# A factorization-machine kernel on one core: the bias addition moves from VectorE to ScalarE and GpSimd, and one transfer of squares is asked for four slots later

## The chip, the cores and the metric

The kernel runs on one core of one Trainium2 chip. The metric is the device time of one execution in microseconds; the time before is the median of 3 runs. A profile is one further execution, taken by the hardware profiler. The engines are named as in the profile: PE is TensorE (PEld its weight loads), DVE is VectorE, ACT is ScalarE, POOL is GpSimd, SP is SyncE. GpSimd and SyncE also ask for DMA transfers; a transfer asked for by GpSimd stands in GpSimd's own order of instructions.

## What is computed

A batch of 1024 vectors of 512 features goes through a linear layer and through 64 embedding matrices of 512 x 512; the squares of the products are summed over the 64 matrices, and a second term with squared inputs and weights is taken off:

```python
out_lin = x @ lin_w.T + lin_b
xv = jnp.einsum('bf,efm->bem', x, weight)
zp = jnp.einsum('bf,efm->bem', jnp.square(x), jnp.square(weight))
interaction = 0.5 * jnp.sum(jnp.square(xv) - zp, axis=1)
return out_lin + interaction
```

All of it is float32. The kernel keeps twice the result, `2 * (x @ lin_w.T + lin_b) + sum of squares`, in two accumulators and takes the half at the end, which is why the bias enters doubled.

## The kernel before

**Tiling.** The 64 matrices are worked through in 16 blocks of four (q = 0 to 15). Products are formed by a two-level fast scheme with seven products instead of eight. The outer level has seven operand matrices "1", "2", "6", "7", "5", "3", "4" for each block, in this order (`UNITS`). Each of them has two column halves j = 0, 1, and each such unit (line 413) makes seven inner products on TensorE, "1", "5", "6", "2", "7", "3", "4", into three PSUM banks x, v and y. A block has thus 7 x 2 x 7 = 98 products, each of them two profiled matmul pieces of 128x512.

**Slots and order.** Everything is put into one list with a due time in slots (`st.at(t, fn)`), sorted by it and then issued in that order, by hand. One slot is one inner product, a block takes 98 slots, and block q starts at slot 98q. Each engine runs its own instructions in that order; a fraction of a slot only sets the order. So an instruction that waits holds back all later ones of its engine, and for GpSimd that includes the transfers it asks for.

**What GpSimd does.** It forms the differences of weights for the scheme: outer ones on line 380 (`outer_t`), inner ones on lines 391, 393 and 395 (`inner_t`, called tp, t6 and t4 in this order for each operand matrix). TensorE reads these. On line 472 (`rest`) it does additions of 128x1024 for operand "5", at slots 67 and 69.8 of a block for j = 0, and 74 and 76.8 for j = 1; these wait for VectorE's last `join` (line 467) into tile s. On line 506 (`gather`) it asks for the transfers that add squares from z tiles into an accumulator, and on line 522 for those that sum squared weights.

**What VectorE does.** It takes the products out of PSUM: lines 446, 457, 458 and 467 each add a bank and an SBUF tile. TensorE writes the banks again, so it waits for these reads: product "4" goes into bank y after `join("y", 3)` on line 467 has read it.

**Accumulators and squares.** The result has four blocks of quarters, named by z tiles: place "a", "b" and "c" (`place`, line 407). ScalarE squares them in place (line 497). The accumulators `acc0` and `acc1` are 128 x 2 x 2 x 512 each, indexed by j, then by column half s. In each block these transfers go into them (slot in the block, j, half u of the tile):

- c into acc0: 38.8 (u 0) and 52.9 (u 1), both j together, 1024 KB each
- c into acc1: 73 and 84 (j 0), 80 and 91.5 (j 1), 512 KB each
- a into acc0, called C12 in the change: 88 (j 0, u 0), 96.5 (j 1, u 0), 99.5 (j 0, u 1), 110.3 (j 1, u 1), 512 KB each
- b into acc1: 111.3 and 124.2, both j together, 1024 KB each

A number above 98 falls into the next block. Each transfer reads and writes the accumulator, so one into a part waits until the earlier one into the same part has landed: 99.5 waits for 88. The last block has its own ending for a and b (lines 741 to 751). Places a and c change their tiles with each block, so a tile that holds a in one block is written as c by VectorE in the next.

**The bias.** A row of 512 numbers is loaded to all partitions (line 350, 256 KB). The addition on VectorE, line 348, is one operation for each accumulator, j and s: eight in all, two in each of blocks 1 to 4, at slots 27.6 (acc0) and 41.6 (acc1):

```python
for n in range(4):
    for r, t in enumerate((27.6, 41.6)):
        st.at(98 * (n + 1) + t, lambda r=r, n=n: add_bias(r, n // 2, n % 2))
```

Of the kernel before, what the change touches and what calls it, by code (L numbers as in the profile page):

```python
# [9 lines left out]
AF = mybir.ActivationFunctionType  # L10
ALU = mybir.AluOpType
# [17 lines left out]
def kernel(  # L29
# [31 lines left out]
    nc = tc.nc  # L61
    _, _, _, Q = x.shape
    E, F, M = weight.shape
    P = 128
# [16 lines left out]
    acc = [  # L81
        const.tile([P, 2, 2, M], F32, tag=f"acc{r}", name=f"acc{r}") for r in range(2)
    ]
# [26 lines left out]
    st = Stream()  # L110
# [232 lines left out]

    bias = const.tile([P, M], F32, tag="bias", name="bias")

    def add_bias(r, j, s):
        o = acc[r][:, j, s]
        nc.vector.scalar_tensor_tensor(o, bias, 2.0, o, ALU.mult, ALU.add)  # L348

    st.at(-1, lambda: nc.sync.dma_start(bias, lin_b.partition_broadcast(P)))  # L350

    for n in range(4):
        for r, t in enumerate((27.6, 41.6)):
            st.at(98 * (n + 1) + t, lambda r=r, n=n: add_bias(r, n // 2, n % 2))

    def load_w(q, kk, v):
        src = weight[4 * q + 2 * v : 4 * q + 2 * v + 2]
        nc.sync.dma_start(
            WB[kk][v], src.rearrange("u (p k) m -> p u k m", k=NK)[:, :, ts(kk, 2)]
        )  # L360
# [12 lines left out]
    def outer_t(i, u):  # L373
        a, b = {
            "5": (WB[0][1], WB[0][0]),
            "6": (WB[1][1], T5),
            "7": (WB[1][1], WB[0][1]),
            "4": (WB[1][0], T6),
        }[i]
        nc.gpsimd.tensor_sub(OUTER[i][:, u], a[:, u], b[:, u])  # L380
# [3 lines left out]
    def inner_t(q, i, n):  # L384

        b = OUTER[i]
        k = 2 if n == "tp" else 1
        t = tpool.tile([P, k, M], F32, tag=n, name=f"{n}_{q}_{i}")
        TI[q, i, n] = t
        if n == "tp":  # L390
            nc.gpsimd.tensor_sub(t, b[:, 1], b[:, :, 0])  # L391
        elif n == "t6":
            nc.gpsimd.tensor_sub(t[:, 0], b[:, 1, 1], TI[q, i, "tp"][:, 0])
        else:
            nc.gpsimd.tensor_sub(t[:, 0], b[:, 0, 1], TI[q, i, "t6"][:, 0])  # L395
# [96 lines left out]
    def squares(t, q, n, j, wait):  # L492
        z = place(q, n)
        for u in range(2):
            st.at(
                t + max(wait, 0.1) * u,
                lambda u=u: nc.scalar.activation(z[:, u, j], z[:, u, j], AF.Square),  # L497
            )
# [3 lines left out]
    def gather(t, q, n, r, j, u):  # L502
        def fn():
            z = place(q, n)[:, u]
            o, z = (acc[r], z) if j is None else (acc[r][:, j], z[:, j])
            nc.gpsimd.dma_start(o, z, accum_op=ALU.add)  # L506

        st.at(t, fn)

    def w_squares(t, q, v, u):  # L510
        first = q == v == u == 0

        def sq(kk):
            o = (w2_sum if first else w2_sb)[:, ts(kk, 2)]
            nc.scalar.activation(o, WB[kk][v][:, u], AF.Square)

        for kk in range(2):
            st.at(t + 0.1 * kk, lambda kk=kk: sq(kk))
        if not first:
            st.at(  # L520
                t + (3.2 if t < 0 else 5),
                lambda: nc.gpsimd.dma_start(w2_sum, w2_sb, accum_op=ALU.add),
            )
# [11 lines left out]
    for q in range(NQ):  # L535
        g0 = 98 * q
        last = q == NQ - 1
        for kk, v, t in ((1, 0, -41), (0, 0, -37.5), (0, 1, -37), (1, 1, -3)):
            if q:
                st.at(g0 + t, lambda q=q, kk=kk, v=v: load_w(q, kk, v))  # L540

        for i, t0, t1 in (
            ("5", -9.9, 2) if q else ("5", -11, -10.9),
            ("6", 14.2, 14.3) if q else ("6", 0.5, 0.6),
            ("7", 28.7, 28.8),
            ("4", 50, 53),
        ):
            for u, t in enumerate((t0, t1)):
                st.at(g0 + t, lambda i=i, u=u: outer_t(i, u))
        for i, *times in (  # L550
            ("1", -6.4, -1.4, 2.1) if q else ("1", -11.5, -11.4, -11.3),
            ("2", 6.4, 6.5, 10.2) if q else ("2", -5, -4.9, -4.8),
            ("6", 20.7, 20.8, 27),
            ("7", 34.4, 34.5, 39.7),
            ("5", 43.1, 43.2, 43.3),
            ("3", 57.9, 58, 61.7),
            ("4", 81, 82.1, 84.1),
        ):
            for n, t in zip(("tp", "t6", "t4"), times):
                st.at(g0 + t, lambda q=q, i=i, n=n: inner_t(q, i, n))  # L560
        for n, (i, (addend, dst)) in enumerate(UNITS.items()):
            for j in range(2):
                unit(g0 + 14 * n + 7 * j, q, i, j, addend, dst)

        for k, n, r, times in (
            (1, "c", 0, ((None, 38.8), (None, 52.9))),
            (4, "c", 1, ((0, 73), (0, 84), (1, 80), (1, 91.5))),
            (5, "a", 0, ((0, 88), (0, 99.5), (1, 96.5), (1, 110.3))),
            (6, "b", 1, ((None, 111.3), (None, 124.2))),
        ):  # L570
            for j in range(2):
                t = g0 + 14 * k + 7 * j + 14.6
                squares(t - (0.95 if last and n == "b" else 0), q, n, j, 4 * (k == 4))
            for m, (j, t) in enumerate(times):
                if not last or n == "c":
                    gather(g0 + t, q, n, r, j, m % 2)
        if q == 0:
            w_times = (-6, 14.8, 37, 56.6)
        else:
            w_times = (-19.2, 14.8, 37, 56.6)  # L580
        for n, t in enumerate(w_times):
            w_squares(g0 + t, q, n // 2, n % 2)
# [249 lines left out]
```

## Time and profile before

| | |
|---|---|
| median of 3 runs | 1425.74 us (1425.23 to 1425.85) |
| profiled execution, its own time | 1423.9 us |
| span of the profile | 1422.1 us |
| granted TensorE clock, mean | 0.996 |
| VectorE busy, share of the span | 893.6 us, 63% |
| ScalarE busy, share of the span | 620.8 us, 44% |
| HBM read, written | 72.61 MB, 2.10 MB |
| line 348, eight operations | 1.37 to 5.67 us each, from 138.3 to 414.0 us |
| line 472, 64 operations | 2.36 us mean |
| line 506, waits for an earlier transfer | 62.7 us in 15 waits, the longest 4.8 |

The span is the time from the first to the last instruction of the profile; the execution's own time has a little more around it. "Busy" counts the time in instructions, so an instruction that is held up while it runs counts as busy too. A name such as `y L421 <- z L467` in a list of waits says: the instruction on line 421 that writes y waited for the one on line 467 that writes z. In a timeline each line has the start and the duration in us, the engine, the line of the kernel, the operation, output `<-` inputs, the shape, the count, and in brackets the idle time before it with what ended it.

### The profile page before, as it was taken

How to read it: one execution, taken by the hardware profiler on the slowest of the kernel's cores; microseconds unless marked ns; L12 is line 12 of the kernel's file. 1: busy time of each engine (PE TensorE's matmuls, PEld its weight loads, DVE VectorE, ACT ScalarE, POOL GpSimd, SP SyncE). 2: the span in 40 equal slices, each digit the busy share in tenths (PEclk: the TensorE clock that was granted, in tenths of full speed). 3: DMA queues.
4: the chain of work that ended last, by engine and by line, in shares of the span. 5: the costliest groups of instructions: out<-in, count | busy, mean ns of one | idle time of the engine just before them, and what ended most of it. 6: DMA issues, size and time to landing. Idle time of an engine off the chain costs nothing.

```text
span 1422.1 us, 11166 instructions
## 1 busy us (share of the span) xinstructions
PE 1407.7 (99%) x3340; PEld 636.5 (45%) x3340; DVE 893.6 (63%) x1271; ACT 620.8 (44%) x824; POOL 1248.8 (88%) x812
## 2 busy tenths in 40 slices
PE   9999999999999999999999999999999999999999
PEld 5444444444444444444444444444444444444446
DVE  6665667657576565665656566565666656566665
ACT  2444353443534435344443534534353443534443
POOL 7988789888898888979989898988989988898984
PEclk9999999999999999999999999999999999999999
DMA  5299898898888998997998899898998998899885
GB/s 214 59 222 191 200 197 160 200 195 195 197 163 206 196 206 193 182 238 156 230 195 197 204 181 234 166 232 178 191 233 160 225 195 211 186 184 237 163 189 133
DMA packets 58108, 273.63 MB, mean 192 GB/s; under 512 B 5440, under 2 KB 8000, under 8 KB 41792
## 3 DMA queue, kind: packets, MB, share of 16 engines
q0 software_dynamic: 36432, 198.20, 71.1%
q1 hardware_dynamic: 21328, 74.19, 15.3%
q10 hardware_dynamic: 288, 0.52, 0.1%
q8 instruction: 27, 0.44, 0.1%
q14 instruction: 33, 0.27, 0.1%
HBM read 72.61 MB, written 2.10 MB: 53 GB/s over the span
## 4 chain that ended last, share of the span: by engine, by line
PE 94%; DMA 2%; issue 1%; POOL 1%; DVE 1%; ACT 0%; POOLq 0%
PE y L421 39%; PE x L421 26%; PE v L421 25%; DMA acc<-z 2%; PE lin L216 1%; PE y_last L659 1%; DVE acc L348 1%; PE v_last L659 0%; PE x_last L659 0%; POOL t L380 0%; PE y_lin L271 0%; DMA t<-lin_wT 0%; POOL t L395 0%; PE v_lin L271 0%; PE x_lin L271 0%
## 5 line engine op out<-in xcount | busy, mean ns | idle before, releaser
L421 PE MATMUL y<-t,xs 128*128 128x512 f32 x896 | 424.0, 594 | 10.3 <-DVE z L467 9.6
L475 ACT COPY y<-x 128x512 f32<-128x512 f32 x224 | 127.7, 570 | 623.1 <-PE x L421 623.0
L467 DVE TENSOR_TENSOR z<-y,s 128x512 f32<-128x512 f32 x192 | 132.7, 691 | 238.0 <-PE y L421 238.0
L421 PEld LDWEIGHTS y<-t,xs 128*128 128x128 f32 x896 | 169.7, 190 | 226.7 <-issue 202.8
L506 POOL DMA_DIRECT2D acc<-z x190 | 213.2, 1153 | 64.3 <-DMA acc<-z 62.7
L497 ACT ACTIVATE z<-z 128x1024 f32<-128x1024 f32 x256 | 260.1, 1054 | 11.8 <-POOL z L472 9.3
L421 PE MATMUL x<-w,xs 128*128 128x512 f32 x512 | 252.0, 600 | 0.0
L421 PE MATMUL y<-tp,xs 128*128 128x512 f32 x448 | 229.1, 593 | 0.0
L421 PE MATMUL v<-tp,xs 128*128 128x512 f32 x448 | 228.8, 592 | 0.0
L472 POOL TENSOR_TENSOR z<-z,s 128x1024 f32<-128x1024 f32 x64 | 149.6, 2355 | 50.7 <-DVE s L467 50.7
L421 PE MATMUL x<-t,xs 128*128 128x512 f32 x384 | 188.3, 592 | 0.0
L391 POOL TENSOR_TENSOR tp<-w 128x1024 f32<-128x1024 f32 x64 | 175.2, 2738 | 13.9 <-PE y L421 12.6
L467 DVE TENSOR_TENSOR z<-v,s 128x512 f32<-128x512 f32 x192 | 132.8, 691 | 72.2 <-PE v L421 70.6
L458 DVE TENSOR_TENSOR z<-y,z 128x512 f32<-128x512 f32 x192 | 132.4, 690 | 57.4 <-PE y L421 57.4
L380 POOL TENSOR_TENSOR t<-w,t 128x1024 f32<-128x1024 f32 x64 | 164.1, 2725 | 0.0
L458 DVE TENSOR_TENSOR z<-x,z 128x512 f32<-128x512 f32 x192 | 132.3, 689 | 37.3 <-PE x L421 35.7
L421 PEld LDWEIGHTS x<-w,xs 128*128 128x128 f32 x512 | 98.4, 192 | 123.8 <-issue 123.5
L391 POOL TENSOR_TENSOR tp<-t 128x1024 f32<-128x1024 f32 x48 | 139.5, 2906 | 0.0
L421 PEld LDWEIGHTS y<-tp,xs 128*128 128x128 f32 x448 | 85.6, 191 | 107.8 <-issue 107.8
L421 PEld LDWEIGHTS v<-tp,xs 128*128 128x128 f32 x448 | 85.1, 190 | 107.3 <-issue 104.2
L421 PE MATMUL v<-w,xs 128*128 128x512 f32 x256 | 130.7, 592 | 0.0
L446 DVE TENSOR_TENSOR s<-v,z 128x512 f32<-128x512 f32 x160 | 110.6, 691 | 27.8 <-PE v L421 27.1
(113 smaller groups left out, 1485.0 us busy)
## 6 DMA issues: line engine op xcount, KB each, us to landing
w<-weight SPq DMA_DIRECT2D x64, 1024.0 KB, 12.8
acc<-z POOLq DMA_DIRECT2D x128, 512.0 KB, 8.5
w_sum<-w_sb POOLq DMA_DIRECT2D x63, 1024.0 KB, 10.2
acc<-z POOLq DMA_DIRECT2D x62, 1024.0 KB, 8.7
w<-x SPq DMA_DIRECT2D x2, 1024.0 KB, 10.2
out<-z SPq DMA_DIRECT2D x7, 256.0 KB, 2.3
xs<-x SPq DMA_DIRECT2D x2, 384.0 KB, 6.9
t<-lin_wT ACTq DMA_DIRECT2D x2, 256.0 KB, 4.2
```

Of the source, the lines that this page charges most:

```text
L216: nc.tensor.matmul(LIN[n], quarter(0, kk, (0, 1, 3, 2)[2 * s + l])[:, ts(j, P)], lw_sb[:, 2 * kk + l, :], start=(kk == 0 and l == 0), stop ...
L348: nc.vector.scalar_tensor_tensor(o, bias, 2.0, o, ALU.mult, ALU.add)
L380: nc.gpsimd.tensor_sub(OUTER[i][:, u], a[:, u], b[:, u])
L391: nc.gpsimd.tensor_sub(t, b[:, 1], b[:, :, 0])
L421: nc.tensor.matmul(d[bank], xsl(i, o)[:, ts(j, P)], operand_b(q, i, o), start=start, stop=True, skip_group_check=True,)
L446: nc.vector.tensor_add(o, d[bank], zblk(q, addend, j, b))
L458: nc.vector.tensor_add(zblk(q, dst, j, b), d[bank], zblk(q, addend, j, b))
L467: nc.vector.tensor_add(s if both else zblk(q, dst, j, b), d[bank], s)
L472: nc.gpsimd.tensor_add(place(q, n)[:, 1, j], place(q, src)[:, 1, j], d["s"])
L475: st.at(t0 + 0.5, lambda: nc.scalar.copy(d["y"], d["x"]))
L497: lambda u=u: nc.scalar.activation(z[:, u, j], z[:, u, j], AF.Square),
L506: nc.gpsimd.dma_start(o, z, accum_op=ALU.add)
```

## The change

The bias is doubled once, in place, by ScalarE at slot 21 of the first block. The addition goes to GpSimd: one operation covers both column halves s of an accumulator and j, with the bias row read twice (a broadcast). There are four of them instead of eight, one in each of blocks 1 to 4, at slot 64.5: acc0 with j 0 and 1 in blocks 1 and 2, acc1 with j 0 and 1 in blocks 3 and 4. Besides, the transfer of a into acc0 with j 0 and u 1 goes from slot 99.5 to slot 103.5, in all blocks but the last.

```diff
-    def add_bias(r, j, s):
-        o = acc[r][:, j, s]
-        nc.vector.scalar_tensor_tensor(o, bias, 2.0, o, ALU.mult, ALU.add)
+    def add_bias(r, j):
+        o = acc[r][:, j]
+        nc.gpsimd.tensor_add(o, o, bias.unsqueeze(1).broadcast_to([P, 2, M]))
 
     st.at(-1, lambda: nc.sync.dma_start(bias, lin_b.partition_broadcast(P)))
+    st.at(21, lambda: nc.scalar.activation(bias, bias, AF.Copy, scale=2.0))
 
     for n in range(4):
-        for r, t in enumerate((27.6, 41.6)):
-            st.at(98 * (n + 1) + t, lambda r=r, n=n: add_bias(r, n // 2, n % 2))
+        st.at(98 * (n + 1) + 64.5, lambda n=n: add_bias(n // 2, n % 2))
...
-            (5, "a", 0, ((0, 88), (0, 99.5), (1, 96.5), (1, 110.3))),
+            (5, "a", 0, ((0, 88), (0, 103.5), (1, 96.5), (1, 110.3))),
```

On GpSimd the addition stands directly ahead of line 472's first operation in its block. The moved transfer stands behind two operations that it was ahead of: line 380 (`outer_t("5", 1)`, slot 2 of the next block) and line 395 (t4 of matrix "1", slot 2.1). It passes no other transfer, and SyncE's list is the same in both kernels.

## The prediction, made before the changed kernel had run

> **What bounds the kernel now.** I read the page first, to see which engine has no room:
>
> ```profile
> PE 1407.7 (99%) x3340; PEld 636.5 (45%) x3340; DVE 893.6 (63%) x1271; ACT 620.8 (44%) x824; POOL 1248.8 (88%) x812
> ```
>
> TensorE (PE) is busy for 1407.7 of 1422.1 us, and the chain of waits gives it 94%. An edit on another engine can therefore only pay by closing holes in PE, or cost by opening new ones. So next the waits of PE alone (columns: total us, times, longest us):
>
> ```profile
> PE y L421 <- DVE z L467: 9.6, 4, 2.7
> PE y L421 <- POOL t L395: 0.7, 1, 0.7
> ```
>
> Four holes of 2.3 to 2.7 us end with VectorE (DVE), one ends with GpSimd (POOL). Four is also the number of embedding blocks that have bias additions on VectorE. The timelines of the three engines around the first hole (columns: start, us):
>
> ```profile
> 152.86 1.02 PE L421 MATMUL y<-t,xs 128*128 128x512 f32 x2
> 156.20 1.20 PE L421 MATMUL y<-t,xs 128*128 128x512 f32 x2 [2.32 <-DVE z L467]
> 157.19 3.55 PE L421 MATMUL x<-w,xs 128*128 128x512 f32 x4
> 160.58 1.02 PE L421 MATMUL y<-tp,xs 128*128 128x512 f32 x2
> ```
>
> ```profile
> 150.24 5.31 DVE L348 SCALAR_TENSOR_TENSOR acc<-bias,acc 128x512 f32<-128x512 f32 x1
> 155.47 0.68 DVE L467 TENSOR_TENSOR z<-y,s 128x512 f32<-128x512 f32 x1
> ```
>
> ```profile
> 150.22 1.56 POOL L395 TENSOR_TENSOR t<-w,t 128x512 f32<-128x512 f32 x1
> 151.44 1.18 POOL L522 DMA_DIRECT2D w_sum<-w_sb  x1
> 152.04 2.94 POOL L391 TENSOR_TENSOR tp<-t 128x1024 f32<-128x1024 f32 x1
> 155.07 1.61 POOL L393 TENSOR_TENSOR t<-t,tp 128x512 f32<-128x512 f32 x1
> ```
>
> The bias addition on line 348 starts 0.02 us after a GpSimd operation and ends only after the next GpSimd operation is over (155.55 against 154.98); the GpSimd operation after that takes 1.61 us instead of the usual 1.27. L467 stands queued behind it on VectorE and must read bank y before PE may write it again. The list of the operations on tile acc shows that this is waiting, not work (min/median/max in ns; L713 is the same kind and shape at the end of the kernel, when GpSimd is idle):
>
> ```profile
> L348 DVE SCALAR_TENSOR_TENSOR acc<-bias,acc x8: 1371/3518/5667, 138.3 to 414.0; 128x512 f32<-128x512 f32 x8
> L713 DVE SCALAR_TENSOR_TENSOR z<-acc,z x6: 684/685/692, 1409.5 to 1413.8; 128x512 f32<-128x512 f32 x6
> ```
>
> Taken one by one, the four additions to acc0 take 1.37 to 1.75 us and hurt nobody; the four to acc1 take 5.28 to 5.67 us, and each one is followed by a hole in PE.
>
> [...] the addition with two SBUF inputs takes 5.3 us beside GpSimd and 0.685 us without it, while those with one PSUM input stay at 0.69 us. [...] four matmul pieces at 157.19 need 3.39 us until the next start, against 1.72 us elsewhere; and the third hole, at 329.63, has no such slow stretch.
>
> **Part 1: eight additions leave VectorE.** I price this by the period of a block. The first L472 of a block waits for VectorE's result of a fixed matmul, so its start marks PE's progress. The starts are 87.81, 176.21, 264.58, 351.28, 440.14 and 524.26 us. The periods are 88.40, 88.37, 86.70 and 88.86 us in the four blocks with bias, then 84.12 us. The excesses are 4.28 + 4.25 + 2.58 + 4.74 = 15.85 us. The first one checks against the PE lines above: 3.34 instead of 0.86 us (2.48), 0.99 instead of 0.86 (0.13), 3.39 instead of 1.72 (1.67), together 4.28. Of the fourth, 0.31 us belongs to part 3 (386.29 to 388.32 us, 2.03 instead of 1.72). So 15.54 us leave with the additions. Next late after them is nothing: in the blocks after 440 us, which have no addition, PE runs through the same places without a hole.
>
> **Part 2: four GpSimd additions and one ScalarE doubling arrive.** ScalarE does one 128x512 operation, 0.57 us by its copies (L475), at about 49 us, before a copy that it waits 5.44 us for: nothing. The value arrived long before (the bias load was issued at 9.9 and took 13.5 us). Each GpSimd addition is 128x1024 with two SBUF inputs. The nearest rows are 2.36 us (L472) and 2.95 us (L380)[...]. In the changed program it stands directly ahead of the first L472 of blocks 1 to 4. That is the one place in the block where GpSimd has a whole hole:
>
> ```profile
> 764.67 0.86 POOL L506 DMA_DIRECT2D acc<-z  x1
> 772.34 1.56 POOL L395 TENSOR_TENSOR t<-w,t 128x512 f32<-128x512 f32 x1
> 776.61 4.68 POOL L472 TENSOR_TENSOR z<-z,s 128x1024 f32<-128x1024 f32 x2 [2.70 <-DVE s L467]
> 807.79 0.88 POOL L506 DMA_DIRECT2D acc<-z  x1 [4.35 <-DMA acc<-z]
> ```
>
> From 773.90 to 776.61 there are 2.7 us: 2.36 fits, 2.95 sticks out by 0.25, and the second L472 pair has 0.55 us of waiting ahead of it to take that up. The addition also brings a wait. In blocks 1 and 2 it needs the transfer into acc0 asked for at 764.67, which lands 8.1 us later (8.0 in blocks 1 to 4), at 772.8: 1.1 us early. In blocks 3 and 4 its transfer into acc1 landed long before. Queued behind it are L472, two transfers and then tp of operand 4 (787.86 to 790.51 us), which PE reads at 791.88: 1.37 us of slack, with the 0.55 together 1.9 us. So the addition could end at 778.5, after 4.6 us, before PE noticed. Cost taken: 0. Bounds: 0 and, if it were held as long as VectorE's was (5.3 us), 0.7 us four times, 2.8 us.
>
> **Part 3: the transfer moves 4 slots, in every block but the last.** In the last view above GpSimd stands 4.35 us until the transfer asked for at 794.15 has landed (13.4 us). In the new order L380 and L395 come ahead of the moved transfer; no other transfer is passed, and SyncE's queue is the same. L393 ends at 803.4, so L380 and L395 run to about 807.3, the transfer waits some 0.5 us and is issued at 807.8, as now. So the DMA traffic keeps its times, and GpSimd's next tp starts 3.5 us earlier (808.4 instead of 811.95; PE reads it at 815.91). What matters is L395, operand t4 of matrix 1: it now ends at 812.29, and PE needs it at 812.48 (second pair of the four y pieces that start at 811.62). With 0.2 us of slack every longer landing shows in PE: at 962.87 it was 13.8 us, the wait 4.83 us, and the period 85.04 (+0.92); the next has 84.20 (+0.08), and block 4 its 0.31. Sum 1.31 us, which goes, because L395 no longer stands behind the wait. Below nothing: the transfer reads a tile that VectorE overwrites at 822.12; with 6.5 to 8.1 us to land it is done by 816. Being issued even 4 slots (4 x 84.12/98 = 3.4 us) later than now would still leave 2.8 us. Cost 0.
>
> **Sum.** 15.54 + 1.31 = 16.85 us. The profiled execution took 1423.9 us for a span of 1422.1, so 1407.05 by its own clock. The median of the runs is 1425.74, 1.84 us above that execution; I take the difference off the median: 1408.9 us.
>
> **Rivals.**
> - GpSimd becomes the late engine (B): the addition is held up as VectorE's was. For it speaks GpSimd's 88%; against it that VectorE keeps no operation with two SBUF inputs there. 2.8 us come back: 1411.7.
> - The moved transfer brings nothing, since its wait is the same landing (C): for it speaks that the issue time hardly moves; against it the order, which takes L395 out. 1.31 us stay: 1410.2.
> - Slower (D): the moved transfer lands so late that VectorE's first write into the tile (822.12) waits, and PE behind it, in 15 blocks. It starts at a landing of 14.3 us after 807.8; at 16 us it costs 15 x 1.7 = 25 us: 1425.7 - 16.9 + 25 = 1434. To end slower than now by 0.2% it needs 15.6 us. Against it: this transfer lands in 6.5 to 8.1 us in all fifteen blocks, and the longest of all 190 took 14.1.
> - The additions weren't held by GpSimd but by a landing (E): then the wait moves to GpSimd with them. Against it: the transfer into acc1 asked for at 139.07 took 10.2 us, so it had landed at 149.3, before the slow addition began at 150.24. Even so PE only feels what exceeds 4.6 us; it would be inside 0.2%, 1425, only if every stall came back.
>
> **How the numbers follow.** Forecast 0.77, B 0.09, C 0.09, E 0.02, D 0.03. The forecast's own bounds are 1407.5 (runs scatter by 0.6) to 1410; B and C are inside 1412. So 1407.0 to 1412.0 leaves out D, E and a little of each side. About 0.2% (2.9 us) is what a measurement here can tell from no change: faster 0.95, within 0.02, slower 0.03.
>
> **What would show it.** Right: no wait of PE for L467; L472 starts 84.1 us apart in all blocks; line 348 on GpSimd at 2.3 to 3.0 us, its hole before L472 shrunk to 0.3 us in four blocks; the wait for the landing near 0.5 us instead of 4. Wrong: PE waiting for L391 or L395 around 792 us of a block with bias, GpSimd standing before line 348, or VectorE waiting for a DMA before L467.

## The result, and the profile after

| | before | after |
|---|---|---|
| median | 1425.6 us (1425.23 to 1425.85, 4 runs) | 1406.18 us (1405.72 to 1406.38, 4 runs) |
| profiled execution, own time / span | 1423.9 / 1422.1 us | 1405.72 / 1403.9 us |
| GpSimd waits for a landing (line 506) | 62.7 us, 15 times | 11.0 us, 16 times |

The ratio is 0.9864 (95% interval 0.9846 to 0.9881), so the change makes the kernel 1.4% faster. The forecast was 1408.9 us with a range from 1407.0: the direction is right and the time lies 0.8 us below the range. The gain is 19.4 us where 16.85 were worked out. The mechanism can be read from the profile after; where the other 2.6 us come from took more profiles of the kernel before.

The waits of PE, the whole list (total us, times, longest):

```profile
PE y_spin L202 <- PEq L821: 0.8, 1, 0.8
PE lin L216 <- DMA t<-lin_wT: 0.3, 1, 0.3
```

Neither L467 nor L395 is left in it; both remaining lines belong to the start. The page's chain of waits says the same:

```profile
PE 99%; DMA 0%; DVE 0%; issue 0%
```

The timeline of GpSimd in block 1 (start, duration, idle before), where the new addition stands:

```profile
166.37 1.56 POOL L395 TENSOR_TENSOR t<-w,t 128x512 f32<-128x512 f32 x1
167.61 2.62 POOL L348 TENSOR_TENSOR acc<-acc,bias 128x1024 f32<-128x1024 f32 x1
170.62 4.69 POOL L472 TENSOR_TENSOR z<-z,s 128x1024 f32<-128x1024 f32 x2 [0.38 <-DVE s L467]
```

The addition follows L395 at once, so the transfer it depends on had landed, and its 2.62 us fill the 2.7 us hole up to 0.38 us. L472 still waits for VectorE at the end, so its start isn't later. The same timeline at a moved transfer:

```profile
785.46 3.13 POOL L380 TENSOR_TENSOR t<-w,w 128x1024 f32<-128x1024 f32 x1
787.78 2.04 POOL L395 TENSOR_TENSOR t<-w,t 128x512 f32<-128x512 f32 x1
790.53 0.87 POOL L506 DMA_DIRECT2D acc<-z  x1 [0.72 <-DMA acc<-z]
791.14 2.66 POOL L391 TENSOR_TENSOR tp<-w 128x1024 f32<-128x1024 f32 x1
```

L380 and L395 now come first and the wait has shrunk to 0.72 us. The starts of the first L472 of each block are 84.11 or 84.12 us apart in all 15 periods.

### The profile page after: what moved, and what is told of

Read it like the earlier page. It is cut to its first block, busy times and chain, and to the rows that moved or that the text cites. A ratio compares the mean times of both kernels' runs of the same rounds, so it can differ in the third digit from the quotient of the medians.

```text
span 1403.9 us, 11169 instructions
## 1 busy us (share of the span) xinstructions
PE 1399.7 (100%) x3340; PEld 634.8 (45%) x3340; DVE 869.0 (62%) x1263; ACT 620.9 (44%) x825; POOL 1257.8 (90%) x816
## 4 chain that ended last, share of the span: by engine, by line
PE 99%; DMA 0%; DVE 0%; issue 0%
PE y L421 41%; PE v L421 27%; PE x L421 27%; PE lin L216 1%; PE y_last L659 1%; PE x_last L659 0%; PE v_last L659 0%; PE y_lin L271 0%; DMA t<-lin_wT 0%; PE v_lin L271 0%; PE x_lin L271 0%; PE end L722 0%; DVE z L732 0%
## 5 line engine op out<-in xcount | busy, mean ns | idle before, releaser
L467 DVE TENSOR_TENSOR z<-y,s 128x512 f32<-128x512 f32 x192 | 132.6, 691 | 242.9 <-PE y L421 242.9
L421 PE MATMUL x<-w,xs 128*128 128x512 f32 x512 | 248.4, 592 | 0.0
L391 POOL TENSOR_TENSOR tp<-w 128x1024 f32<-128x1024 f32 x64 | 174.9, 2734 | 23.8 <-PE y L421 22.6
L472 POOL TENSOR_TENSOR z<-z,s 128x1024 f32<-128x1024 f32 x64 | 149.6, 2354 | 42.7 <-DVE s L467 42.7
L467 DVE TENSOR_TENSOR z<-v,s 128x512 f32<-128x512 f32 x192 | 132.6, 691 | 72.5 <-PE v L421 71.0
L380 POOL TENSOR_TENSOR t<-w,t 128x1024 f32<-128x1024 f32 x64 | 164.2, 2728 | 0.0
L391 POOL TENSOR_TENSOR tp<-t 128x1024 f32<-128x1024 f32 x48 | 130.0, 2708 | 19.2 <-PE y L421 19.1
```

Of the source, the lines that this page charges most:

```text
L421: nc.tensor.matmul(d[bank], xsl(i, o)[:, ts(j, P)], operand_b(q, i, o), start=start, stop=True, skip_group_check=True,)
L467: nc.vector.tensor_add(s if both else zblk(q, dst, j, b), d[bank], s)
L472: nc.gpsimd.tensor_add(place(q, n)[:, 1, j], place(q, src)[:, 1, j], d["s"])
```

## The experiments

**The kernel before, three more profiles.** Two theories for the missing 2.6 us: chance in the kernel before (theory 1), or something outside the blocks that the change shortens for good (theory 2).

> The kernel before, once more, with several executions. 2.6 us of the gain (19.4 measured, 16.85 worked out) are still without a cause. Theory 1, a term of chance in the kernel before: in the profiled execution the third of the four holes had no stretch of slow matmuls after it (period 86.70 instead of 88.4), so that execution was 1.7 us better than the typical one, 1423.9 against 1425.6. Then this profile shows four periods of 88.3 to 88.9 in blocks 1 to 4 and an own time near 1425.6; if one of the four is short by some 1.7 us again, the own time is lower by the same. Theory 2, the change makes something else shorter for good (the head, or the tail): then the four periods are again as in the first profile (15.85 us over 4 x 84.12), own time 1423.9, and the difference to the changed kernel lies outside the periods.

> The kernel before, a third profile. If chance in the slow stretches behind the four holes is what makes its times differ (1420.8 to 1427.0 in 19 runs), then the own time follows from the periods: 1405.9 (a changed kernel's time) plus the sum of the excesses over 84.12 us, within 1 us, which is how the first start-up differs. Each hole costs 2.5 to 2.9 us without a slow stretch and 4.2 to 4.9 with one. A typical run of 1425.4 shows four with one.

> The kernel before, a fourth profile, for the same sum: own time minus the excesses over 84.12 us is again 1405.4 to 1407.1. If it isn't, there is a term outside the four blocks with bias that the sum doesn't hold.

The kernel before turned out to vary much more than its first three runs showed: in 19 more runs it took 1420.78 to 1427.0 us, median 1425.05, and in 14 runs under the name before_again 1420.97 to 1426.13, ratio 0.9998 (0.9988 to 1.0008). Against 1425.05 the gain of the change is 18.9 us, not 19.4. The reason for the scatter is in the timeline of PE of before_again, first block 1, then block 2:

```profile
155.03 1.12 PE L421 MATMUL y<-t,xs 128*128 128x512 f32 x2 [2.30 <-DVE z L467]
156.00 1.88 PE L421 MATMUL x<-w,xs 128*128 128x512 f32 x4
157.71 1.02 PE L421 MATMUL y<-tp,xs 128*128 128x512 f32 x2
...
241.84 1.30 PE L421 MATMUL y<-t,xs 128*128 128x512 f32 x2 [2.42 <-DVE z L467]
242.93 3.44 PE L421 MATMUL x<-w,xs 128*128 128x512 f32 x4
246.21 1.02 PE L421 MATMUL y<-tp,xs 128*128 128x512 f32 x2
```

Both holes are alike (2.30 and 2.42 us). Behind the first the four pieces of x take 1.71 us from start to start, behind the second 3.28. Pieces at that slower pace are called a slow stretch here. The table by stretches shows the granted clock beside it (from the left: stretch and length; busy us of PE, its weight loads, VectorE, ScalarE, GpSimd; clock; DMA share; GB/s):

```profile
130.00:175.00 45.00, 42.70 (x100) 18.68 (x100) 32.74 (x42) 14.05 (x20) 39.37 (x25) 1.00 0.92 197
220.00:260.00 40.00, 37.58 (x85) 16.25 (x84) 29.91 (x37) 12.13 (x16) 34.53 (x23) 0.96 0.88 191
```

A hole costs about its own length, and in 14 of the 16 cases of four profiles a slow stretch on top. In the first profile blocks 2 and 3 show it:

```profile
244.57 1.12 PE L421 MATMUL y<-t,xs 128*128 128x512 f32 x2 [2.29 <-DVE z L467]
245.54 3.28 PE L421 MATMUL x<-w,xs 128*128 128x512 f32 x4
248.60 1.37 PE L421 MATMUL y<-tp,xs 128*128 128x512 f32 x2
...
332.96 1.12 PE L421 MATMUL y<-t,xs 128*128 128x512 f32 x2 [2.31 <-DVE z L467]
333.93 1.88 PE L421 MATMUL x<-w,xs 128*128 128x512 f32 x4
335.64 1.02 PE L421 MATMUL y<-tp,xs 128*128 128x512 f32 x2
```

Block 2, with a slow stretch, is 4.25 us over 84.12, block 3, without one, 2.58. The sum over whole executions (periods are of the first L472; the excess is what all 15 periods together have over the 1261.75 us that they take in the changed kernel; the last column is own time minus first L472 minus excess):

| profile | first L472 | periods of blocks 1 to 4 | excess | own time | rest |
|---|---|---|---|---|---|
| before, first | 87.81 | 88.40, 88.37, 86.70, 88.86 | 16.87 | 1423.90 | 1319.22 |
| before_again | 86.67 | 86.68, 88.50, 88.39, 89.08 | 17.58 | 1423.46 | 1319.21 |
| before_p3 | 87.15 | 88.39, 88.34, 88.41, 89.08 | 18.71 | 1425.07 | 1319.21 |
| before_p4 | 86.85 | 88.34, 88.42, 88.40, 89.10 | 18.81 | 1424.90 | 1319.24 |
| after | 86.50 | 84.12, 84.12, 84.11, 84.12 | 0.0 | 1405.72 | 1319.22 |

The rest is the same to 0.03 us, so nothing outside the periods and the start-up is concerned: theory 1 holds, theory 2 falls. Two of the four profiles of before have one short period, some 1.7 us shorter than its like in the other profiles. They are the two with an own time of 1423.5 to 1423.9; the two without one took 1424.9 and 1425.07. In this term the prediction's profile was a favourable one. The start-up, the time to the first L472, differs by up to 1.3 us as well (86.50 to 87.81). It lies ahead of every instruction that the change touches: in the first profile PE's first four pieces of `lin` started at 4.67 us and took 2.93 us to the next start, in the profile after they started at 4.44 and took 1.82. From that next start to the first L472 it is 80.20 to 80.24 us in all ten profiles of this document, so the change has no part in it.

**Each part alone.** One has the bias on ScalarE and GpSimd with the transfer at its old slot (the edit is against the changed kernel):

```diff
-            (5, "a", 0, ((0, 88), (0, 103.5), (1, 96.5), (1, 110.3))),
+            (5, "a", 0, ((0, 88), (0, 99.5), (1, 96.5), (1, 110.3))),
```

> The bias on ScalarE and GpSimd, the transfer left at slot 99.5. The prediction's terms give 15.54 us for this part, 17.2 if theory 1 adds 1.7 for the third hole: 1408 to 1410, periods 84.12 in blocks 1 to 4, GpSimd waiting some 4 us in each block before the transfer, and here and there a hole of up to 1 us in PE behind L395 where a landing took over 13.4 us. If the holes came from elsewhere than from the addition on VectorE, the time stays near 1425.

It took 1407.46 us (1407.14 to 1408.04, 4 runs), ratio 0.9885 (0.9869 to 0.9901), 0.5 us below the 1408 to 1410 expected and otherwise as expected. Its periods are 84.12 us but for 84.51 in block 4 and 84.82 in block 11. The timelines of GpSimd and PE in block 11 show why:

```profile
960.69 0.87 POOL L506 DMA_DIRECT2D acc<-z  x1 [4.61 <-DMA acc<-z]
961.30 2.66 POOL L380 TENSOR_TENSOR t<-w,w 128x1024 f32<-128x1024 f32 x1
963.62 1.55 POOL L395 TENSOR_TENSOR t<-w,t 128x512 f32<-128x512 f32 x1
```

```profile
965.23 1.13 PE L421 MATMUL y<-t,xs 128*128 128x512 f32 x2 [0.43 <-POOL t L395]
```

The wait for the landing was 4.61 us instead of the 4.0 of most blocks, and PE stood for L395. The two excesses sum to 1.10 us in this profile, and the medians of this kernel and of the whole change differ by 1.28 us.

The other has the changed slot, and the kernel before's VectorE additions (the edit is against the kernel before):

```diff
-            (5, "a", 0, ((0, 88), (0, 99.5), (1, 96.5), (1, 110.3))),
+            (5, "a", 0, ((0, 88), (0, 103.5), (1, 96.5), (1, 110.3))),
```

> The transfer at slot 103.5, the bias left on VectorE. The prediction's term gives 1.31 us: about 1424.3, the four holes behind L467 as before, no hole behind L395, GpSimd's waits for landings near 10 us in all instead of 63. If the two parts are not additive (GpSimd runs 3.5 us earlier at the start of a block, so the two-input addition meets other GpSimd operations at slot 41.6), the four holes change in length: anything from none to 5 us each.

It took 1417.8 us (1414.38 to 1418.63, 6 runs), ratio 0.9953 (0.9937 to 0.9968): 7.2 us less than before, not 1.3. The second clause of the expectation came true. In the list of VectorE's operations in block 1 the slow addition is now the one to acc0, and the one to acc1 is free:

```profile
137.01 4.62 DVE L348 SCALAR_TENSOR_TENSOR acc<-bias,acc 128x512 f32<-128x512 f32 x1
150.93 0.68 DVE L348 SCALAR_TENSOR_TENSOR acc<-bias,acc 128x512 f32<-128x512 f32 x1
```

GpSimd, being ahead, runs two L380 back to back from 136.12 to 141.07 us, and the addition that came at 137.01 ended at 141.63:

```profile
136.12 4.95 POOL L380 TENSOR_TENSOR w<-w,w 128x1024 f32<-128x1024 f32 x2
141.15 2.70 POOL L391 TENSOR_TENSOR tp<-w 128x1024 f32<-128x1024 f32 x1
...
149.84 0.88 POOL L522 DMA_DIRECT2D w_sum<-w_sb  x1 [0.64 <-ACT w_sb L515]
152.09 2.35 POOL L391 TENSOR_TENSOR tp<-t 128x1024 f32<-128x1024 f32 x1 [1.38 <-PE y L421]
```

During the free addition, from 150.93 to 151.61, GpSimd runs no operation of its own: it has just asked for a transfer and waits for PE until 152.09. The ends of the held additions tell the same. All eight in the first profile of the kernel before and the four slow ones here end 0.55 to 0.57 us after the end of a GpSimd operation.

The holes in PE are 1.7 to 2.4 us instead of 2.3 to 2.7, and in this profile no slow stretch follows any of them (periods 86.08, 86.17, 86.07 and 86.79). The slower runs of the kernel show a mean clock of 0.998 to 0.999, the two fastest 1.0. That a slow stretch follows a shorter hole less often would fit both, but is not shown: one profile has four such holes, and no run varied their length by itself.

**The additions still on VectorE, where GpSimd is idle.** The edit is against the kernel before; the transfer is at slot 103.5 as well, by the edit just shown.

```diff
-        for r, t in enumerate((27.6, 41.6)):
+        for r, t in enumerate((64.6, 64.7)):
```

> The transfer at slot 103.5 and the eight additions still on VectorE, but at slots 64.6 and 64.7, where GpSimd waits 2.7 us for VectorE. If it is GpSimd's two-input operations that hold VectorE's addition, it runs here in 0.69 us or a little more, L467 is late by less than 0.6 us, PE has no hole and the time is that of the changed kernel, 1406.2 within 1 us. If the addition is slow for another reason (a landing, the operation itself), it takes over 1.4 us here too and PE has holes.

It took 1406.19 us (1405.97 to 1406.57, 4 runs), ratio 0.9876 (0.986 to 0.9892), the time of the changed kernel. From the list of line 348 and the timelines of VectorE and GpSimd:

```profile
L348 DVE SCALAR_TENSOR_TENSOR acc<-bias,acc x8: 681/684/685, 169.1 to 422.1; 128x512 f32<-128x512 f32 x8
```

```profile
169.11 1.28 DVE L348 SCALAR_TENSOR_TENSOR acc<-bias,acc 128x512 f32<-128x512 f32 x2
170.31 0.68 DVE L467 TENSOR_TENSOR s<-v,s 128x512 f32<-128x512 f32 x1
```

```profile
166.81 1.56 POOL L395 TENSOR_TENSOR t<-w,t 128x512 f32<-128x512 f32 x1
171.08 4.68 POOL L472 TENSOR_TENSOR z<-z,s 128x1024 f32<-128x1024 f32 x2 [2.71 <-DVE s L467]
```

The same eight operations on the same engine, on the same data, take 0.68 us each while GpSimd stands idle (168.37 to 171.08 us). So what was on the path in the kernel before was not the work of the addition but what GpSimd ran beside it.

**What the addition costs on GpSimd.** Once left out, together with the doubling (the output then lacks the bias), and once put where VectorE had it:

```diff
-    st.at(21, lambda: nc.scalar.activation(bias, bias, AF.Copy, scale=2.0))
...
-    for n in range(4):
-        st.at(98 * (n + 1) + 64.5, lambda n=n: add_bias(n // 2, n % 2))
```

> The changed kernel without the doubling and the four additions, so the bias is left out of the output. If the addition on GpSimd costs nothing in its place, this takes the same 1406.2 within 0.6 us. If it costs anything (as the bound of 2.8 us allowed), this is faster by that.

```diff
-        st.at(98 * (n + 1) + 64.5, lambda n=n: add_bias(n // 2, n % 2))
+        st.at(98 * (n + 1) + (27.6, 41.6)[n // 2], lambda n=n: add_bias(n // 2, n % 2))
```

> The four additions on GpSimd, but not in its hole: at slots 27.6 (acc0) and 41.6 (acc1), where VectorE had them, between the operand differences; the transfer at slot 103.5. The prediction called the hole before L472 the one place with room. If so, some operand is 2.6 us late in each of the four blocks and PE waits for L391, L393 or L395: up to 2 us each plus the slow stretch, 1408 to 1420. Rival: the moved transfer lets GpSimd run 3.5 us ahead there (it waits 41.6 us for PE before L391 in the changed kernel, 1.5 us a time), so that 2.6 us fit here too: 1406.2 within 0.6, the waits before L391 shorter in four blocks.

Both ratios are against seven more runs of the kernel before, with a median of 1423.16 us. Without the bias: 1406.69 us (1406.09 to 1406.98, 4 runs), ratio 0.9883 (0.9865 to 0.99), no faster than with it. Its median is 0.5 us above the changed kernel's, but its 15 periods are 84.11 or 84.12 too; in its profile the first operation of `rest` came at 87.78 us instead of 86.50, which is chance in the start-up. At the old slots: 1406.39 us (1405.87 to 1407.08, 4 runs), ratio 0.9882 (0.9867 to 0.9897), no slower, with the same periods. So the forecast of 1408 to 1420 failed there, and the rival of that expectation holds: GpSimd's waits for PE before L391 fell from 41.6 us in all in the changed kernel (first line) to 34.4 (second line):

```profile
POOL tp L391 <- PE y L421: 41.6, 30, 1.5
POOL tp L391 <- PE y L421: 34.4, 26, 1.5
```

The additions wait for nothing at these slots. One to acc1, in block 3, starts with no idle time before it:

```profile
315.14 1.57 POOL L395 TENSOR_TENSOR t<-w,t 128x512 f32<-128x512 f32 x1
316.38 2.65 POOL L348 TENSOR_TENSOR acc<-acc,bias 128x1024 f32<-128x1024 f32 x1
```

So the hole before L472 was not the one place with room. With the transfer moved, GpSimd has room between the operand differences too. Whether it would also fit there with the transfer at slot 99.5 was not tried.

## Why the prediction was right, and where it failed

- *What bounds the kernel* held: PE without holes is 84.12 us a block, and all of the gain in the periods came from closed holes and the slow stretches behind them.
- *Part 1, the additions leave VectorE.* Shown as a cause by the additions placed in GpSimd's idle time, which run in 0.68 us, by the first part alone, and by part2_only, where the same additions are slow or free as GpSimd's operations lie. Rival E, a landing, falls: the held additions end 0.55 to 0.57 us after GpSimd's operations, and on GpSimd at the old slots none waits for a landing (there the moved transfer had shifted GpSimd's issues, so this alone would not settle it). The runs show that this float32 addition with two SBUF inputs is held beside GpSimd's operations, 5.3 us against 0.68. By what they hold it, and why L467, with one PSUM input, takes 0.68 us beside GpSimd's L393 (from 155.47 us in the first profile), the runs do not show.
- *Part 2, at no cost.* Right in time. The addition took 2.63 us, between the two rows named (2.36 and 2.95), and doubling it on ScalarE 0.63 us; leaving both out gained nothing. Its statement that this is the one place with a whole hole is true of the block that it showed. In blocks 1 and 2 of the same profile, where PE was late, GpSimd also stood 3.40 and 3.16 us before L391, and the last experiment shows that the hole was not needed. Rival B falls.
- *Part 3, the moved transfer.* As the second of two parts it is worth about what the prediction gave it, so rival C falls: 1.28 us by the medians and 1.10 by the periods of one profile, against 1.31. That the medians agree to 0.03 us is luck, as start-ups alone scatter by more. The wait of the moved transfers is some 0.7 us (0.47 to 1.16) where some 0.5 were forecast. What the prediction didn't see is that alone it is worth 7.2 us, since it shifts GpSimd against VectorE's additions. Against the median of 1425.05 the two parts alone gain 17.6 and 7.2 us, and the whole 18.9: they partly close the same holes. The slower rival D did not occur.
- *The sum is the step that failed*, in two of its terms. It said "The median of the runs is 1425.74, 1.84 us above that execution; I take the difference off the median". That treats the difference as a fixed offset, while the 16.85 us come from that very execution. Its third block had no slow stretch and its excess was 2.58 us instead of the 4.2 to 4.3 of a typical one. The term for part 1 was 15.54 us and is some 17.4 where all four holes have their slow stretch (before_p3: 4.27 + 4.22 + 4.29 + 4.96, less the 0.31 that was given to part 3). The second term, the start-up, was put at nothing without a word; it was 1.31 us shorter in the profile after, by chance. By execution the account closes: 1423.90 less 16.87 less 1.31 is 1405.72, the time measured. Of the 2.7 us between the forecast and the median, 1.84 are the offset: without it the sum says 1407.05. The other 0.9 us are of the size by which start-ups scatter; which start-ups the median runs had is not on record. The range missed it because its lower bound reckoned with 0.6 us of scatter, the spread of three runs, while 19 runs of the kernel before spread over 6.2 us.
- The prediction saw the sign of this itself, when it noted that the third hole had no slow stretch, and did not carry it into the sum.
- *The slow stretches.* Holes of 2.3 to 2.7 us had one behind them in 14 of the 16 cases in four profiles, and each cost some 1.7 us (3.39 against 1.72 us for four pieces of x in the first profile). What decides whether one follows is not shown: in that profile none followed the hole of 2.31 us, while one followed those of 2.29 and 2.32.

## What to carry to other kernels

When a hole on the bounding engine ends with another engine, look at what a third engine was running: here an operation that took 5.3 us in one place and 0.68 in another was held, not working, and moving it in time was worth as much as moving it to another engine (1406.19 against 1406.18 us). Price a hole by the period of the loop rather than by its length, and over several profiles: here what followed a hole of 2.3 us cost some 1.7 us more, and did not come every time. Take the expected gain from the execution in which it was counted, and compare that execution with the median term by term before using the difference as an offset.

## What the runs showed that was not expected

- A kernel with four holes of under 3 us in PE scattered over 6.2 us (1420.78 to 1427.0 in 19 runs); the four kernels without such holes over 1.4 us (1405.72 to 1407.08 in 16 runs).
- The start-up differs by up to 1.3 us between executions (first L472 at 86.50 to 87.81 us), with the start and the pace of the first four pieces of `lin`. In all ten profiles the own time less the first L472 and the excess is 1319.20 to 1319.24 us.
- Placing one transfer four slots later in the order, and nothing else, made another of VectorE's additions the slow one: 0.68 us instead of 5.3 for acc1, 4.6 instead of 1.4 for acc0. The transfer itself was asked for at about the same time as before; what came earlier were GpSimd's operations behind it.
